# The third map set of a gateless tick moves behind the rounds

## The chip, the cores and the metric

The kernel runs on one core of one Trainium2 chip. The metric is the device time of one execution in microseconds (us); the figure given is the median of several runs. Engines are named as the profile names them: PE (matmul), PEld (weight load), DVE, ACT, POOL and SP, which here only starts transfers.

## What is computed

The input `x` is 8 images of 8 channels and 512 x 512 points in float32. Two layers follow each other, each of the form x + f(group_norm(x)). Layer 0 is a spectral convolution on a grid of half the resolution that keeps 4 x 4 modes. Layer 1 has three branches and a blend of them:

```python
grid = drive                                  # 1: "map", 15 steps, each channel by itself
for _ in range(15):
    mapped = R * grid * (1.0 - grid)
    local = conv3x3_per_channel(mapped, K_local)
    grid = (1 - BETA) * ((1 - EPS) * mapped + EPS * local) + BETA * drive
cml = clip(grid, 1e-4, 1 - 1e-4)
h = relu(conv3x3(x, Wp) + bp)                 # 2: "nca", 8 -> 128 channels
nca = sigmoid(conv1x1(h, Wu) + bu)            #    128 -> 8 channels
gin = concat(x, cml, nca)                     # 3: "gate", 24 -> 8 -> 8 channels
g = sigmoid(conv1x1(relu(conv3x3(gin, Wg1) + bg1), Wg2) + bg2)
out = x + g * cml + (1 - g) * nca
```

## The kernel before, in words

An image is an *element*. Its work is cut into small pieces, and the source issues the pieces in an order written out by hand; the last call of the kernel (`keep_order`) makes every engine follow the order of the source. The unit of that order is the *tick*, one call of `turn` (L1145), which calls `work` (L1084).

**Map sets.** The rows of an image are cut into overlapping slabs of 32 rows, so that 15 steps can run in on-chip memory. A set (`Slabs`, L493) holds 16 slabs of one channel or pairs of four channels: the state `m`, and two layouts of the drive, `dE` for even and `dO` for odd steps. Nine sets make an element: four sets of channels 0 to 3 (first phase), then four of channels 4 to 7 and a `Tail` set (second phase). The list `slots` orders them: step 1 of every set of the phase, step 2 of every set, and so on. A tick takes `TICK` = 3 slots. One slot is

- `convolve` (L541): 48 matmuls in the source, 96 in the trace, into one *half* of the accumulators. There are two halves of two tiles `pair` each, and `half()` (L1088) takes them in turn.
- `settle` (L554): DVE adds the drive to one tile of the half (L560), ACT squares the result (L566), then both again for the other tile. It is a generator that stops before the second square. The square, and what follows it, run when it is next called: the drive's own preparation on POOL after step 1 (`drive(0)`, L539), the release of a drive tile at steps 14 and 15 (`sets.drop(d)`), the clip at step 15 (L619), and `renew` (L578), which exchanges edge rows between neighbouring sets by four transfers that POOL starts (L593, L594).

**Rounds.** `Hidden.round` (L738) makes four rows of `h`: 24 matmuls in the trace (L746) into a half, then ACT evicts one tile of it (L752) and DVE the other (L754). A tick has one to three rounds. The second call of the last set's `settle` lies in the first round.

**Channel sums.** `Hidden.point` (L769) multiplies the new rows of `h` by `Wu`, 8 matmuls a round in the trace (L773), and collects four rounds in a tile `y`: the first group of them is copied by ACT (L780), later ones are added by DVE (L782), and the fourth is followed by a sigmoid (L785) and a store (L788). When a tick's rounds fall into two groups of four, there are two calls, into the two sides of the same tile `pair`.

**Gates and spectral pieces.** A gate (`Gate`, L795) does 12 rows of the blend of the element before, and a *piece* is a step of layer 0 for the element after. A tick takes them up where they are due, around the sums.

**A tick before the change**, in the order of every engine: three map sets; then `transfers` (L1105); then the rounds; `squares` (L1114); then sums, gate and pieces; then `tick()`, which issues stores put off (the map's result, `cml`, L623), and `squares` again.

**Transfers and slots.** `transfers` (L1149) issues on SP, in this order, the store of `y`, up to two loads of 1 MB of the next image (`x`, L184), and the loads of the drives of the next phase (`Phase.fetch`, L710; four loads of 256 KB a tile, L518). A drive tile is loaded only if

```python
if not h and sets.room() <= begun - self.squared or len(s.e.closed) < C:
    break
```

lets it pass: `room()` is the number of free slots, `begun` counts the sets of the phase that have begun, and `squared` those whose state exists. The slots are 19 in all, of which 16 are for sets in the last four ticks of a phase. `square` (L520) makes the state from `dE` on ACT (L525) and takes a slot. `prepare` (L698) calls `drive(1)` at the start of a tick, four instructions on POOL (L539) that scale `dO` in place; it takes a tile that was loaded in an earlier tick. Step 1 of a set reads `dO`.

Of the kernel before, what the change touches and what calls it, by code (L numbers as in the profile page):

```python
# [54 lines left out]
TICK = 3  # L55
WIDE, EARLY, FILL, LATE, LAST = "wide", "early", "fill", "late", "last"
# [63 lines left out]
def conv_layers(ctx: ExitStack, tc: tile.TileContext, a, out):  # L120
# [45 lines left out]
    def later(ticks, work):  # L166
        put_off.append((now[0] + ticks, work))

    def tick(end=False):
        now[0] += 1  # L170
        due = [w for at, w in put_off if end or at <= now[0]]
        put_off[:] = [] if end else [(at, w) for at, w in put_off if at > now[0]]
        for work in due:
            work()
# [504 lines left out]
    class Phase:  # L679
# [23 lines left out]
        def squares(self, n):  # L703
            while self.squared < len(self.sets) and sets.room():
                if not self.ready(self.squared, 0, n + TICK):
                    break
                self.sets[self.squared].square()
                self.squared += 1
# [86 lines left out]
    class Gate:  # L795
# [59 lines left out]
        def finish(self):  # L855

            x1, o = (self.mix[: GR * C, q] for q in range(2))
            nc.vector.scalar_tensor_tensor(  # L858
                o, o, self.e.back[: GR * C, 0:1], x1, ALU.add, ALU.add
            )  # L860
            self.store()
# [71 lines left out]
    class Others:  # L933
# [52 lines left out]
        def busy(self):  # L986
            ahead = self.loaded or self.begun
            return self.before.gates or ahead or self.convolved or self.pointed

        def finish(self):  # L990
            while self.pointed:
                self.pointed.popleft().finish()
# [64 lines left out]
    others = Others()  # L1057
    for n in count():
# [6 lines left out]
        ps = next(turns)  # L1065
# [18 lines left out]
    def work(steps, rounds, e, after, gates, transfers, squares=lambda: None):  # L1084

        double = gates == 2 and not others.lag

        def half():  # L1088
            used[0] += 1
            return halves[used[0] % 2]  # L1090

        settled = iter(())
        for n, (s, step) in enumerate(steps):
            ps = half()
            s.convolve(step, ps)
            next(settled, None)
            settled = s.settle(step, ps)
            next(settled)
            others.finish()
            if gates == 2 and shared.most < 6:  # L1100
                others.load(1)
                gates = 1
        if steps:
            others.finish()
        transfers()  # L1105
        if steps:
            had = len(others.loaded) + len(others.begun)
            others.load(gates, early=True)
            gates -= len(others.loaded) + len(others.begun) - had
        for _ in range(rounds):  # L1110
            e.hidden.round(half(), after, settled)
        next(settled, None)
        others.finish()
        squares()  # L1114


        first, second = halves[used[0] % 2], halves[(used[0] + 1) % 2]
        if not others.spectral(WIDE, second):
            used[0] += 1
            first, second = second, first  # L1120
        groups = e.hidden.sums()
        gate = others.ready()
        if not gate:
            others.spectral(EARLY, [first[0][:, 0]])
        if len(groups) == 2:
            e.hidden.point(groups.pop(0), first[1][:, 0])
        two = False
        if gate:
            others.conv(first[0][:, 0])
            others.spectral(EARLY, [second[0][:, 0]])  # L1130
            two = others.ready(double)
            if two:
                others.conv(second[0][:, 0])
        if groups:
            e.hidden.point(groups[0], first[1][:, 1])
        others.spectral(FILL, [None])
        others.spectral(LATE, [second[1][:, 0]])
        others.point()
        others.spectral(LAST, [first[1][:, 0]])
        used[0] += two  # L1140
        others.load(gates)
        tick()
        squares()
# [26 lines left out]
    for b in range(B):  # L1170
# [3 lines left out]
        done, rounds = e.hidden.n, ROUNDS if after else ROUNDS_LAST  # L1174
        first, second = phases[2 * b : 2 * b + 2]
# [98 lines left out]
```

## Time and profile before

| what | value |
|---|---|
| median of 3 runs | 9159.09 us (9153.91 to 9171.87) |
| the profiled execution's own time | 9170.25 us |
| its span, first to last instruction | 9168.5 us |
| mean granted TensorE clock | 0.991 |
| PE busy | 8748.3 us (95%) |
| DVE busy | 5628.9 us (61%) |
| ACT busy | 4099.4 us (45%) |
| POOL busy | 3383.3 us (37%) |
| map matmuls, L547 | x103680, 3681.8 us |
| round matmuls, L746 | x24576, 2779.2 us |
| sum matmuls, L773 | x8192, 996.2 us |

Busy times are unions of the instructions' spans. In the views of groups, a row has the line, the engine, the operation, what it writes and reads, its shape and count, then the busy time and the mean duration of one, then the idle time of that engine just before, with what ended most of it. In a timeline a row is the start (us from the first instruction), the length, engine, line, operation, operands and count of instructions merged into it, and in brackets the idle time before it and what ended it. "issue" means that nothing in the profile explains the idle time.

### The profile page before, as it was taken

The numbers are of one execution on the slowest core, as the hardware profiler recorded it, in microseconds if no ns is written. First come the engines' busy times: TensorE is split into PE (matmuls) and PEld (weight loads), VectorE is DVE, ScalarE is ACT, GpSimd is POOL, SyncE is SP. The second block draws the span as 40 slices with busy tenths as digits, with TensorE's granted clock in tenths as the row PEclk, the third lists the DMA queues.
The fourth block names the chain that finished last, engine by engine and source line by source line (L and its number), as shares of the span: only waits on it lengthen the run. The fifth ranks groups of instructions, "written<-read, shape, count | busy, mean of one in ns | idle before, by whom it ended". The sixth has DMA issues, their size and how long they took to land. (4 is left out here: it accounts for less than half of the span.)

```text
span 9168.5 us, 334776 instructions
## 1 busy us (share of the span) xinstructions
PE 8748.3 (95%) x150992; PEld 4141.6 (45%) x150992; DVE 5628.9 (61%) x5844; ACT 4099.4 (45%) x4285; POOL 3383.3 (37%) x4470
## 2 busy tenths in 40 slices
PE   5999999999999999999999999999999999999999
PEld 2445544444444444444444444444444444444433
DVE  6665567555675567655676556765567655565654
ACT  2455544444444444444444444444444444444432
POOL 3242434324343243433434334343333434454423
PEclk9999999999999999999999999999999999999999
DMA  5241356745566455754557545565465754755587
GB/s 161 81 133 39 108 138 176 171 110 140 145 179 162 112 157 140 186 143 113 155 150 180 140 113 155 155 174 140 113 164 150 180 135 106 177 138 140 118 209 204
DMA packets 695939, 1327.27 MB, mean 145 GB/s; under 512 B 147648, under 2 KB 153152, under 8 KB 667024
## 3 DMA queue, kind: packets, MB, share of 16 engines
q1 hardware_dynamic: 587376, 1235.73, 52.5%
q0 software_dynamic: 104992, 69.33, 3.5%
q8 instruction: 1187, 19.45, 0.9%
q14 instruction: 240, 1.97, 0.1%
q10 hardware_dynamic: 2144, 0.80, 0.0%
HBM read 977.48 MB, written 270.61 MB: 136 GB/s over the span
## 5 line engine op out<-in xcount | busy, mean ns | idle before, releaser
L547 PE MATMUL pair<-m,band 32*32 32x512 f32 x103680 | 3681.8, 604 | 178.4 <-issue 113.3
L566 ACT ACTIVATE m<-m 128x1024 f32<-128x1024 f32 x2016 | 2128.7, 1056 | 2038.6 <-DVE m L560 1963.9
L547 PEld LDWEIGHTS pair<-m,band 32*32 32x32 f32 x103680 | 2141.5, 103 | 1650.2 <-issue 785.9
L746 PE MATMUL pair<-cols,w_p 32*128 32x511 f32 (+1 forms) x24576 | 2779.2, 597 | 22.9 <-DMA cols<-xn 15.1
L754 DVE TENSOR_SCALAR h<-pair,b_p 128x1024 f32<-128x1024 f32 x1024 | 1313.6, 1283 | 1135.9 <-PE pair L746 1125.8
L593 POOL DMA_DIRECT2D m<-m x1568 | 851.0, 543 | 3087.7 <-ACT m L566 3012.8
L746 PEld LDWEIGHTS pair<-cols,w_p 32*128 32x128 f32 x24576 | 1308.8, 185 | 1501.8 <-issue 1157.3
L560 DVE SCALAR_TENSOR_TENSOR m<-pair,dO 128x1024 f32<-128x1024 f32 x1152 | 1356.2, 1219 | 982.0 <-PE pair L547 791.1
L560 DVE SCALAR_TENSOR_TENSOR m<-pair,dE 128x1024 f32<-128x1024 f32 x1008 | 1186.8, 1219 | 862.3 <-PE pair L547 671.3
L752 ACT ACTIVATE h<-pair,b_p 128x1024 f32<-128x1024 f32 x1024 | 1141.1, 1114 | 1184.9 <-PE pair L746 1174.2
L853 POOL TENSOR_TENSOR mix<-mix 96x512 f32<-96x512 f32 x344 | 437.3, 1277 | 1853.1 <-ACT mix L851 1806.1
L773 PE MATMUL pair<-h,w_u 128*32 128x512 f32 x8192 | 996.2, 596 | 72.3 <-DVE y L782 45.7
L830 PE MATMUL pair<-gin,w_g 128*32 128x511 f32 (+1 forms) x8256 | 951.6, 597 | 21.4 <-DMA gin<-nca 11.7
L594 POOL DMA_DIRECT2D m<-m x1568 | 838.0, 534 | 55.1 <-issue 31.7
L773 PEld LDWEIGHTS pair<-h,w_u 128*32 128x32 f32 x8192 | 246.0, 109 | 684.7 <-issue 523.7
L830 PEld LDWEIGHTS pair<-gin,w_g 128*32 128x32 f32 x8256 | 252.5, 110 | 669.5 <-issue 599.0
L785 ACT ACTIVATE y<-y,b_u 128x512 f32<-128x512 f32 x256 | 184.8, 722 | 727.4 <-DVE y L782 727.4
L835 POOL TENSOR_TENSOR mix<-mix 96x512 f32<-96x512 f32 x344 | 443.7, 1292 | 139.6 <-DMA mix<-nca 86.7
L780 ACT COPY y<-pair 128x512 f32<-128x512 f32 x256 | 149.9, 586 | 641.3 <-PE pair L773 622.7
L570 POOL TENSOR_SCALAR dO<-dO 128x2048 f32<-128x2048 f32 x72 | 398.0, 5527 | 95.3 <-DVE m L560 94.4
L847 PE MATMUL pair<-mix,w_g 128*32 128x512 f32 x2064 | 354.4, 601 | 44.1 <-DVE mix L840 40.6
L840 DVE TENSOR_SCALAR mix<-pair,b_g 128x512 f32<-128x512 f32 x344 | 257.1, 747 | 222.6 <-PE pair L830 213.4
(96 smaller groups left out, 3038.9 us busy)
## 6 DMA issues: line engine op xcount, KB each, us to landing
gin<-xn SPq DMA_DIRECT2D x344, 384.0 KB
x<-in_x SPq DMA_DIRECT2D x120, 1024.0 KB
cols<-xn SPq DMA_DIRECT2D x240, 512.0 KB
gin<-cml SPq DMA_DIRECT2D x344, 320.0 KB
gin<-nca SPq DMA_DIRECT2D x344, 320.0 KB
dE<-xn SPq DMA_DIRECT2D x288, 256.0 KB
dO<-xn SPq DMA_DIRECT2D x288, 256.0 KB
mix<-xn SPq DMA_DIRECT2D x344, 192.0 KB
```

Source lines behind the costliest of these rows:

```text
L547: nc.tensor.matmul(ps[h // 2][32 * t : 32 * t + 32, h % 2], band[at, self.channel(step - 1, h, t), dx], m[at, t, dx : dx + N], start=(n == ...
L560: nc.vector.scalar_tensor_tensor(u[:, at], ps[q], FLOOR, d[:, at], ALU.max, ALU.add)
L566: nc.scalar.square(u[:, at], u[:, at])
L593: nc.gpsimd.dma_start(out=view(tb, rb, dims), in_=view(ta, ra, dims))
L594: nc.gpsimd.dma_start(out=view(ta, ra + s, dims), in_=view(tb, rb + s, dims))
L746: nc.tensor.matmul(ps[g // 2][:, g % 2, lo:hi], w_p[p, dx, i % 2], self.cols[p, i // 2, at : at + hi - lo], start=(n == 0), stop=(n == 2), ...
L752: nc.scalar.activation(h[:, :2], ps[0], AF.Relu, bias=b_p)
L754: nc.vector.tensor_scalar(h[:, 2:], ps[1], b_p, 0.0, ALU.add, ALU.max)
L773: nc.tensor.matmul(ps[32 * g : 32 * g + 32], w_u[:, r % 4], h[:, g], start=(r == hs[0][0]), stop=(r == hs[-1][0]), tile_position=(0, 32 * g),)
L830: nc.tensor.matmul(ps[32 * j : 32 * j + 32, lo:hi], gband[:, dx], gin[:, j, at : at + hi - lo], start=(n == 0), stop=(n == 2), tile_positi ...
L835: nc.gpsimd.tensor_tensor(d, d, ng, ALU.subtract)
L853: nc.gpsimd.tensor_tensor(d, d, mix[: GR * C, 2], ALU.mult)
```

## The change

A tick is *idle* for the other elements when no spectral piece of the element after is left and no gate is loaded and due. In an idle tick of three map sets and at least one round, the third set is taken out of the list and run, with both calls of its `settle` at once, after the rounds and before the second `squares`, the sums and the end of the tick. The sums then always take the half that the last round used, and not the half of the late set.

```diff
@@ class Others
+        def idle(self):
+            return not (self.after and self.after.pieces) and not self.ready()
+
@@ def work
+        late = []
+        if len(steps) == TICK and rounds and not double and others.idle():
+            steps, late = steps[:-1], steps[-1:]
         settled = iter(())
         for n, (s, step) in enumerate(steps):
             ps = half()
...
             e.hidden.round(half(), after, settled)
         next(settled, None)
         others.finish()
+        for s, step in late:
+            ps = half()
+            s.convolve(step, ps)
+            for _ in s.settle(step, ps):
+                pass
         squares()
 
 
         first, second = halves[used[0] % 2], halves[(used[0] + 1) % 2]
-        if not others.spectral(WIDE, second):
+        if late or not others.spectral(WIDE, second):
             used[0] += 1
             first, second = second, first
```

## Prediction, made before the run

> **What bounds the kernel now.** I read first the page's table of busy time:
>
> ```profile
> span 9168.5 us, 334776 instructions
> ...
> PE 8748.3 (95%) x150992; PEld 4141.6 (45%) x150992; DVE 5628.9 (61%) x5844; ACT 4099.4 (45%) x4285; POOL 3383.3 (37%) x4470
> ```
>
> PE is the bound; whatever lengthens its order, or lets it stand, is paid. Then I stepped the source's rules tick by tick. Of 360 ticks with three sets, 60 meet the new condition: 28 in element 0 (the last 28, since no element before it has gates), 4 in each of elements 1 to 6 (one late in the first phase, the last three of the second), 8 in element 7. By rounds and groups of sums: 22 have three rounds in one group, 15 have groups of two and one, 6 of one and two; 14 have two rounds, 3 have one. The timeline of PE shows three of these shapes in a row:
>
> ```profile
> 794.42 9.75 PE L547 MATMUL pair<-m,band 32*32 32x512 f32 x288
> 804.11 8.00 PE L746 MATMUL pair<-cols,w_p 32*128 32x512 f32 x72
> 812.03 2.78 PE L773 MATMUL pair<-h,w_u 128*32 128x512 f32 x24
> 814.75 9.75 PE L547 MATMUL pair<-m,band 32*32 32x512 f32 x288
> 824.43 5.43 PE L746 MATMUL pair<-cols,w_p 32*128 32x512 f32 x48
> 829.78 1.07 PE L773 MATMUL pair<-h,w_u 128*32 128x512 f32 x8
> 831.40 1.06 PE L773 MATMUL pair<-h,w_u 128*32 128x512 f32 x8 [0.56 <-ACT h L752]
> 832.40 9.75 PE L547 MATMUL pair<-m,band 32*32 32x512 f32 x288
> 842.08 8.00 PE L746 MATMUL pair<-cols,w_p 32*128 32x512 f32 x72
> 850.01 1.92 PE L773 MATMUL pair<-h,w_u 128*32 128x512 f32 x16
> 852.83 1.06 PE L773 MATMUL pair<-h,w_u 128*32 128x512 f32 x8 [0.90 <-DVE y L782]
> ```
>
> Three rounds in one group: no wait, 20.33 us a tick. Two rounds: the sums wait 0.56 us for the last eviction, 17.65. Two groups: the second waits 0.90 us for DVE to read the first out of the same tile, 21.43. So all there is to win in clean ticks is 0.56 us in 14 of them and 1.2 in 3. What the late set adds on DVE:
>
> ```profile
> 804.21 2.35 DVE L560 SCALAR_TENSOR_TENSOR m<-pair,dE 128x1024 f32<-128x1024 f32 x2 [0.84 <-PE pair L547]
> ```
>
> The two reads start 0.04 us after the set's last matmul (804.17) and end at 806.56: 2.4 us in which its half isn't free. Last, the transfers before an element's end (SP, POOL, SP):
>
> ```profile
> 2217.13 2.01 SPq L518 DMA_DIRECT2D dE<-xn  x4
> 2220.05 3.50 SPq L518 DMA_DIRECT2D dO<-xn  x4
> ```
> ```profile
> 2232.60 2.72 POOL L539 TENSOR_SCALAR dO<-dO,base 128x512 f32<-128x512 f32 x4 [6.38 <-DMA dO<-xn]
> ```
> ```profile
> 2251.69 4.58 SPq L184 DMA_DIRECT2D x<-in_x  x2
> ```
>
> The last drive tile of the next phase (set 3's dO) is issued until 2223.55; POOL has it at 2232.60, 9.1 us later. SP starts the next image's first two loads at 2251.69, as the element's second tick (2251.83) begins.
>
> [...] The page's queue q8 moved 19.45 MB in 1187 packets, 16.4 KB each[...]. [...] after 2.46 us of waiting (and 0.73 shortly before) three rounds took 10.27 us, not 8.00:
>
> ```profile
> 5595.65 3.09 PE L547 MATMUL pair<-m,band 32*32 32x512 f32 x37 [2.46 <-issue]
> 5598.67 10.27 PE L746 MATMUL pair<-cols,w_p 32*128 32x512 f32 x72
> ```
>
> **The change, part by part.**
>
> *A. The split run of sets.* In single instructions a first set takes 2.82 us to the next, a second 3.12, a third 3.75 to the rounds: 9.69. Split, two take 2.82 + 3.12 + 0.5 (the drain into rounds) = 6.44, and a set alone 2.80 + 0.51 = 3.31: 9.75. The added switch costs 0.07 us a tick.
>
> *B. The new waits.* The next tick's first set takes the late set's half, so it starts no sooner than 2.5 us after the late set ends; and DVE, in order, adds y only after those two reads. Per shape, before to after:
> - three rounds, one group: sums of 2.72 us cover 2.5. +0.07 (the switch) x 22 = 1.5.
> - two rounds: the 0.56 us goes, but sums of 1.8 us leave 0.8 to the half. 17.52 to 17.67 in the commonest tick: +0.15 x 14 = 2.1. One round: the same, +0.05 x 3 = 0.2.
> - groups of two and one: DVE's y (0.69 us) ends 3.1 us after the late set, then 1.14 us to the next set as now: the sums' stretch grows from 3.82 to 4.30. +0.55 x 15 = 8.3.
> - one and two: the y add now comes right after 8 matmuls and 16 follow it: 4.04 to 5.16. +1.19 x 6 = 7.1.
>
> A and B together: **+19 us**. Weight loads and rounds wait for nothing new: each round's half was read out a matmul block earlier, as before. [...]
>
> *C. Transfers move.* The second set's release of its drive tile, in the second call of `settle`, used to run before `transfers`; now it runs in the first round, after it. One slot fewer is seen. I stepped the slots through the last three ticks of a second phase. First: room 2, loads set 0's dO and set 1's dE; now room 1, only dO. Second: room 2, set 1's dO and set 2's dE; now room 3, set 1's dE and dO, then room 1 isn't above begun 2 - squared 1. Third: room 4, squared 3, set 2's dO, set 3's dE and dO; now room 5 but squared 2: set 2's dE, dO, set 3's dE, and then 2 isn't above 4 - 2. So set 3's dO is issued one tick later, in the next element's first tick, behind two image loads, and `drive(1)` for it goes to the start of the second tick. That tick's first set is set 3's step 1, which needs it. By the lines above: SP ends the images at 2256.27, four issues 2.3, then 6.5 to 9.1 us to POOL: 2265 to 2268. Four drives 2.72, DVE 2.4: 2270.2 to 2272.8. The tick's third map set needs that half and would start at 2251.83 + 5.97 = 2257.80. It stands 12.4 to 15 us, say 13.7, and then runs cold for about 2.3 (10.27 - 8.00). **+16 us** at each of the six element boundaries that load an image; at the seventh (7858.6) no image is ahead, I take 13. Sum +109. Unknown is the landing: 10 us a boundary if it lands early, 20[...].
> At the half phases of elements 0 and 7, the same load slips by one tick, ahead of the Tail's two: POOL's drive starts behind the late set's exchange. +3 each, 0 to 6: **+6**.
>
> *D. Gaps that move.* In the 60 ticks PE also stands for instructions and others at the third set (the rows of 5595.65; 6.3 us at 7829, 5 at 8691, 2.7 at 8243, six of 0.5 to 2). [...] Single ticks give 34 us with the cold rounds, of which 17 lie just before a boundary, where C's load fixes the end anyway. I count 0.7 of the other 17: **-12**.
>
> Sum: 19 + 109 + 6 - 12 = +122 on the profiled execution's 9170.25 (span 9168.5 and 1.75 around it): 9292. The runs' median is 11 lower: **9280** after rounding, +1.3%. What is late next at a boundary: the late map set's own release sets the rounds, which follow without a further stop.
>
> **The rivals.** 0.2% is about what a measurement here can tell from no change (18 us).
> 1. *Only the local order counts.* The loads arrive in time, since the DMA share is 0.56 in the first tick of an element (table of stretches, 2234.1 to 2251.8); D gives nothing. 9159 + 19 = 9178. Against it: SP itself stands 6.38 us on a store before the images, so it can't be early.
> 2. *Not slower: the gaps are filled.* [...] all 34 us return, 19 are paid, 9144. It decides only if set 3's dO is driven before about 2257 at each boundary; it needs C to be nil.
> 3. *The condition hardly holds*, say in element 0 alone: 28 ticks of +0.3, about 9168.
> 4. *Worse:* the standing tick pushes gates and later loads, or SP is held a second time: 20 us or more a boundary, 9360.
>
> **Chances.** Forecast 0.78, rivals 0.08, 0.06, 0.02, 0.06. The forecast's own range: 7 x 10 + 10 + 0 - 34 = +46 to 7 x 20 + 28 + 12 = +180, 9205 to 9339; ends that need everything at once are rare, and the local cases lie below, so 9190 to 9335. Faster by over 0.2%: 0.04; within: 0.08; slower: 0.88.
>
> **What would show it.** A: two L547 runs a tick, 192 and 96. B: the bracket before the second L773 group at 1.4 instead of 0.90 (2.2 instead of 1.12 in groups of one and two), and before L547 0.8 after two rounds. C: SP's L518 four times after L184 in the first tick of elements 1 to 6; POOL's L539 dO in the second tick ended by that DMA; PE's L547 idle 12 to 15 us there. If those gaps are under 5 us the prediction is wrong. D: no gap at 7829 and 5584.

## The result and the profile after

| version | median, us | lowest to highest, runs | profiled execution (span) | ratio to before, 95% interval |
|---|---|---|---|---|
| before | 9159.55 | 9153.91 to 9171.87, 4 | 9170.25 (9168.5) | |
| after | 9282.74 | 9275.36 to 9285.35, 4 | 9285.35 (9283.1) | 1.0129, 1.0116 to 1.0141 |

The change makes the kernel 1.3% slower; 9280 had been forecast. The mean granted TensorE clock went from 0.991 to 0.986.

The page of the changed kernel, from the table of busy time:

```profile
PE 8789.2 (95%) x150992; PEld 4093.4 (44%) x150992; DVE 5640.9 (61%) x5844; ACT 4093.4 (44%) x4285; POOL 3375.5 (36%) x4470
```

PE has the same 150992 matmuls and 40.9 us more of busy time, so part of the loss is in matmuls that take longer and the rest in waits. The view of PE's waits names them (what waits for whom: sum in us, times, longest):

```profile
PE pair L547 <- issue: 111.5, 73, 4.7
PE pair L773 <- DVE y L782: 68.2, 35, 2.9
PE pair L547 <- DVE m L560: 66.1, 9, 11.8
```

Before, these three were 113.3, 45.7 and 13.6 (65, 35 and 7 times). Sets that wait for DVE's drive add (L560) are the large new item: 65.4 of the 66.1 us lie in seven waits, one in the second tick of each element but the first. The sums' wait for `y` grew by 22.5 us over the same 35 waits.

**A clean tick.** The timeline of PE, a tick of two rounds and, from 774.79, the start and the second group of sums of a tick of groups of two and one:

```profile
757.73 6.58 PE L547 MATMUL pair<-m,band 32*32 32x512 f32 x192
764.24 5.43 PE L746 MATMUL pair<-cols,w_p 32*128 32x512 f32 x48
769.60 3.41 PE L547 MATMUL pair<-m,band 32*32 32x512 f32 x96
772.93 1.92 PE L773 MATMUL pair<-h,w_u 128*32 128x512 f32 x16
774.79 7.24 PE L547 MATMUL pair<-m,band 32*32 32x512 f32 x192
...
796.45 1.06 PE L773 MATMUL pair<-h,w_u 128*32 128x512 f32 x8 [1.30 <-DVE y L782]
```

The sets stand as 192 and 96. After two rounds the sums run 16 matmuls without a stop (the 0.56 us is gone), but the next run of sets takes 7.24 us, not 6.58. Inside that run its first set waits 0.66 us for the late set's half, which DVE reads until 775.43. The second group of sums waits 1.30 us instead of 0.90.

**An element boundary.** The timelines of SP, POOL and PE around the second tick of the next element, which starts at 2277.87 here and started at 2251.83 before:

```profile
2273.14 1.58 SPq L184 DMA_DIRECT2D x<-in_x  x2
2274.77 3.58 SPq L518 DMA_DIRECT2D dO<-xn  x4
```
```profile
2292.22 2.70 POOL L539 TENSOR_SCALAR dO<-dO,base 128x512 f32<-128x512 f32 x4 [14.92 <-DMA dO<-xn]
```
```profile
2277.87 6.48 PE L547 MATMUL pair<-m,band 32*32 32x512 f32 x180
2287.97 1.08 PE L547 MATMUL pair<-m,band 32*32 32x512 f32 x12 [3.62 <-issue]
2294.90 6.35 PE L547 MATMUL pair<-m,band 32*32 32x512 f32 x96 [5.85 <-DVE m L560]
```

Read from the bottom: the third set starts 17.03 us into the tick (5.97 before) because DVE had no drive to add; POOL had none to scale until 2292.22; and SP issued that load, the four L518, only in the element's first tick, behind two image loads of 1 MB each. The 3.62 us put down to "issue" is a wait for instructions inside the same standing time (the last section has the reason to read it so); without it the wait for DVE is one piece, 10.1 to 11.8 us long at five other boundaries. The set then takes 6.28 us to the rounds (L746 starts at 2301.18), 3.75 before. The tick is 38.09 us long, before 23.77.

**Where the time went.** I cut both traces into ticks and subtracted:

| part of the 114.6 us between the spans | us |
|---|---|
| seven second ticks of elements (12.7 to 14.7 each) | +97.4 |
| 15 idle ticks, groups of two and one | +24.8 |
| 6 idle ticks, groups of one and two | +9.7 |
| 22 idle ticks of three rounds | -11.1 |
| 14 of two rounds | -6.7 |
| 3 of one round | -7.2 |
| all other ticks | +7.8 |

### The profile page after: what moved, and what is told of

The parts are those of the page before. It is cut to its first block, busy times and chain, and to the rows that moved or that the text cites. A ratio compares the mean times of both kernels' runs of the same rounds, so it can differ in the third digit from the quotient of the medians.

```text
span 9283.1 us, 334727 instructions
## 1 busy us (share of the span) xinstructions
PE 8789.2 (95%) x150992; PEld 4093.4 (44%) x150992; DVE 5640.9 (61%) x5844; ACT 4093.4 (44%) x4285; POOL 3375.5 (36%) x4470
## 5 line engine op out<-in xcount | busy, mean ns | idle before, releaser
L547 PE MATMUL pair<-m,band 32*32 32x512 f32 x103680 | 3723.9, 606 | 221.8 <-issue 111.5
L547 PEld LDWEIGHTS pair<-m,band 32*32 32x32 f32 x103680 | 2101.7, 103 | 1769.7 <-issue 837.9
L746 PE MATMUL pair<-cols,w_p 32*128 32x511 f32 (+1 forms) x24576 | 2778.9, 596 | 36.7 <-DMA cols<-xn 14.8
L560 DVE SCALAR_TENSOR_TENSOR m<-pair,dO 128x1024 f32<-128x1024 f32 x1152 | 1356.7, 1219 | 1104.7 <-PE pair L547 775.6
L746 PEld LDWEIGHTS pair<-cols,w_p 32*128 32x128 f32 x24576 | 1303.5, 185 | 1523.6 <-issue 1156.2
L560 DVE SCALAR_TENSOR_TENSOR m<-pair,dE 128x1024 f32<-128x1024 f32 x1008 | 1186.5, 1218 | 886.6 <-PE pair L547 726.8
L773 PE MATMUL pair<-h,w_u 128*32 128x512 f32 x8192 | 998.0, 599 | 87.5 <-DVE y L782 68.2
L830 PE MATMUL pair<-gin,w_g 128*32 128x511 f32 (+1 forms) x8256 | 952.1, 598 | 24.3 <-DMA gin<-nca 14.4
L773 PEld LDWEIGHTS pair<-h,w_u 128*32 128x32 f32 x8192 | 243.0, 110 | 703.9 <-issue 558.6
```

Source lines behind the costliest of these rows:

```text
L547: nc.tensor.matmul(ps[h // 2][32 * t : 32 * t + 32, h % 2], band[at, self.channel(step - 1, h, t), dx], m[at, t, dx : dx + N], start=(n == ...
L560: nc.vector.scalar_tensor_tensor(u[:, at], ps[q], FLOOR, d[:, at], ALU.max, ALU.add)
L746: nc.tensor.matmul(ps[g // 2][:, g % 2, lo:hi], w_p[p, dx, i % 2], self.cols[p, i // 2, at : at + hi - lo], start=(n == 0), stop=(n == 2), ...
L773: nc.tensor.matmul(ps[32 * g : 32 * g + 32], w_u[:, r % 4], h[:, g], start=(r == hs[0][0]), stop=(r == hs[-1][0]), tile_position=(0, 32 * g),)
L830: nc.tensor.matmul(ps[32 * j : 32 * j + 32, lo:hi], gband[:, dx], gin[:, j, at : at + hi - lo], start=(n == 0), stop=(n == 2), tile_positi ...
```

## The experiments

Theory: nearly all of the loss comes from the release of a drive tile that slips past `transfers`, and so from one load a boundary. Rivals: the loss comes from the new order on PE itself; or from the queue order on SP, images ahead of the load. The first four share one chip, on which before took 9165.02 us; the last two share another, with 9168.25.

| kernel | median, us (runs) | ratio to before, 95% interval | PE's L547 waits for DVE's m | PE's L773 waits for DVE's y |
|---|---|---|---|---|
| release first | 9187.61 (17) | 1.0028, 1.0021 to 1.0035 | 0.6 us | 67.9 us |
| one slot fewer | 9311.20 (4) | 1.0161, 1.0148 to 1.0175 | 124.8 | 45.8 |
| drive before images | 9259.23 (4) | 1.0105, 1.0091 to 1.0118 | 41.4 | 68.2 |
| release first, two tiles | 9158.18 (13) | 0.9990, 0.9981 to 0.9998 | 0.6 | 25.5 |
| two tiles only | 9150.23 (13) | 0.9983, 0.9974 to 0.9991 | 10.5 | 25.5 |
| late at the end, two tiles | 9142.67 (13) | 0.9976, 0.9968 to 0.9984 | 10.9 | 25.5 |

**1. The release first.** The changed kernel, with the second set's second `settle` call put back ahead of `transfers`. The late set stays behind the rounds. The call brings the set's second square and its edge exchange forward too, and not the release alone; the second experiment changes the slots alone.

```diff
         if steps:
             others.finish()
+        if late:
+            next(settled, None)
         transfers()
```

> The changed order of the sets, but the second set's settle is finished before the transfers, so that they see the slots that they saw before. If the late load is the cause of the loss (theory): the seven stalls of 12 to 15 us in an element's second tick are gone, set 3's dO is issued in the last tick of the element before, and the time is 9160 to 9185 us, some 100 us under the changed kernel. If the order of the sets itself, or the wait for its half, costs the time (rival): 9250 us or more.

Measured: 1.0028; the median of 9187.61 us is 3 us above the range that was given. The profiled execution took 9179.38 us. Of the seven boundary stalls nothing is left (the seven ticks differ from before by 7.2 us in all, not 97.4). The same boundary, SP's last drive loads and then PE:

```profile
2239.39 4.65 SPq L518 DMA_DIRECT2D dO<-xn  x4
...
2266.20 4.60 SPq L184 DMA_DIRECT2D x<-in_x  x2
```
```profile
2272.60 10.49 PE L547 MATMUL pair<-m,band 32*32 32x512 f32 x288
```

The drive is issued 22 us ahead of the images again, and the three sets of the second tick run as one. Two lines of source take the ratio from 1.0129 to 1.0028. What stays, 23 us by the medians, comes with the rest of the new order. Its profiled execution is only 9 us over that of before: its idle ticks have +21.1 in groups of two and one, +8.8 in one and two, and -21.3 in the others. The profiled execution is 8 us under this version's median and that of before 5 us over its own on this chip, which makes up the difference. Which ticks vary from run to run is open, for there is one profile of each.

**2. One slot fewer, old order.** The kernel before, with nothing moved, but `transfers` sees one free slot fewer in those idle ticks in which the second set is at step 14 or later.

```diff
+        fewer = 0
+        if len(steps) == TICK and rounds and not double and others.idle():
+            fewer = int(steps[1][1] >= STEPS - 1)
...
+        sets.most -= fewer
         transfers()
+        sets.most += fewer
```

> The order of before, unchanged; only the transfers of the idle ticks whose second set is at step 14 or 15 see one slot fewer, as in the changed kernel. Theory: the load slips as in the changed kernel, seven stalls of 12 to 15 us, 9250 to 9275 us. Rival (the order costs the time): within 10 us of before.

Measured: 1.0161, more than the change itself. The direction is as expected; the size is not (9250 to 9275 us had been given). SP and PE at the boundary, whose second tick starts at 2273.85:

```profile
2276.42 1.91 SPq L184 DMA_DIRECT2D x<-in_x  x2
2278.39 3.63 SPq L518 DMA_DIRECT2D dO<-xn  x4
```
```profile
2297.53 6.87 PE L547 MATMUL pair<-m,band 32*32 32x512 f32 x96 [17.10 <-DVE m L560]
```

The images are issued 2.57 us into the tick, where the changed kernel has them 4.73 us ahead of it, and the third set starts at +23.68 instead of +17.03. The seven ticks lose 132.8 us. So the slot alone makes the stall, without any late set. The late set even shortens it: SP's load of `cols` (L729) starts within 0.1 us of the end of a tick's rounds at this boundary in all three versions, and the stores ahead of the images follow it. In the changed kernel the late set and the sums come after that point, so it lies 25.3 us ahead of the second tick; 20.6 us here, 20.2 us before.

**3. The drive before the images.** The changed kernel; a drive load that slipped into the next element is issued ahead of that tick's images.

```diff
+            for p in now_phases:
+                if at >= p.at:
+                    p.fetch(at)
             if others.after:
                 others.after.fetch()
             for p in now_phases:
-                p.fetch(at)
+                if at < p.at:
+                    p.fetch(at)
```

> The changed kernel, but a drive load that is still due when its phase has begun is issued on SP ahead of the two image loads. Theory: at six boundaries 2 MB less lie ahead of set 3's dO[...]; POOL's drive starts 6 to 7 us after the last issue instead of 14, the stall falls from about 12 to 5 us, and the cold stretch shrinks: 9225 to 9250 us. Rival (the load is late because of the stores ahead of it, or POOL is late for another reason): within 10 us of the changed kernel.

Measured: 1.0105, 23 us under the changed kernel by the medians and above the range of 9225 to 9250 us that was given; the seven boundary ticks give back 28 us. SP and POOL, where the second tick starts at 2274.07:

```profile
2271.24 3.09 SPq L518 DMA_DIRECT2D dO<-xn  x4
2274.50 1.12 SPq L184 DMA_DIRECT2D x<-in_x  x2
```
```profile
2284.68 2.70 POOL L539 TENSOR_SCALAR dO<-dO,base 128x512 f32<-128x512 f32 x4 [11.17 <-DMA dO<-xn]
```

The last of the four loads is issued at +0.26 us (+0.48 in the changed kernel): SP gained almost nothing, since the store of `nca` holds it for 8.53 us here too. What shrank is the way from that issue to POOL, 10.35 us instead of 13.87. It had been expected to shrink to 6 or 7 us. So the images ahead in the queue cost 3.5 us at this boundary (over the six boundaries that load an image the third set starts 4.8 us sooner in the mean); the rest of the stall comes with the slipped tick itself.

**4. Two tiles for the two groups.** The kernel of experiment 1, and the second group of sums goes to the half's other tile, so that it need not wait until DVE has read the first.

```diff
-            e.hidden.point(groups[0], first[1][:, 1])
+            e.hidden.point(groups[0], first[0][:, 1] if late else first[1][:, 1])
```

> e1_release_first, and in ticks with a late set the second group of sums goes to the other tile of the half, so that it doesn't wait for DVE to read the first. Theory (the added wait in ticks of two groups is DVE's y behind the late set's two reads): 21 ticks lose 1.3 to 2.4 us each, 25 to 40 us under e1_release_first, 9125 to 9150 us. Rival (the next set's wait for its half takes the place of that wait at once): within 10 us of e1_release_first.

Measured: 0.9990, 29 us under the kernel of experiment 1. The absolute time lies above the range that was given, the step is as expected. A tick of groups of two and one, PE:

```profile
788.48 2.78 PE L773 MATMUL pair<-h,w_u 128*32 128x512 f32 x24
791.19 6.58 PE L547 MATMUL pair<-m,band 32*32 32x512 f32 x192
```

All 24 matmuls of the sums run without a stop. PE's wait for `y` falls from 67.9 to 25.5 us, 42 us; in its one profile 20 us of that come back as waits for instructions (93.3 to 113.8 us).

**5. Two tiles only.** The same edit in the kernel before, without a late set.

```diff
+        alone = len(steps) == TICK and not double and others.idle()
...
-            e.hidden.point(groups[0], first[1][:, 1])
+            e.hidden.point(groups[0], first[0 if alone else 1][:, 1])
```

> The kernel before with no late set; only in ticks without gate and pieces the second group of sums goes to the other tile. Theory (PE waits 0.9 to 1.1 us there for DVE to read a tile of which the other side is free): 21 ticks lose 1.1 to 1.4 us, 20 to 27 us in all, 9130 to 9142 us, ratio about 0.997. Rival (the next map sets wait for the second tile instead): within 5 us of before.

Measured: 0.9983, 18 us under before, less than expected. The wait for `y` goes from 45.7 to 25.5 us, so that 20 us was to be had. With the late set (0.9990, experiment 4) the kernel is not seen to be faster than without it; the two intervals overlap, so no gain of the late set beyond the second tile is shown.

**6. The late set where gaps are.** The kernel of experiment 5; the late set runs behind the rounds only in the last tick of each second phase (`Tail` at step 15), with the release first as in experiment 1. The diff shows the new condition, against the kernel before; the late loop is that of the change. The trace of before has long waits for instructions in several of these ticks (2.46 us at 5595.65 among them).

```diff
+        late = []
+        alone = len(steps) == TICK and rounds and not double and others.idle()
+        if alone and isinstance(steps[-1][0], Tail) and steps[-1][1] == STEPS:
+            steps, late = steps[:-1], steps[-1:]
```

> e5_two_tiles_only, and the late set only in the last tick of each element's second phase (8 ticks), its releases as before. Theory (there PE stands for instructions during the third set, up to 6 us with a cold clock behind it, and the rounds give them time): 10 to 20 us under e5_two_tiles_only, 9112 to 9130 us. Rival (the instructions or transfers that are late there are late in the next tick instead): within 5 us of e5_two_tiles_only, or above it.

Measured: 0.9976, the lowest ratio of all, 7.6 us under the kernel of experiment 5, where 10 to 20 had been expected; the intervals of the two overlap, so the size of that step is unsure. The last tick of element 1, first in the kernel of experiment 5 and then here, PE:

```profile
2208.80 1.75 PE L547 MATMUL pair<-m,band 32*32 32x512 f32 x7 [4.91 <-issue]
```
```profile
2206.71 2.13 PE L547 MATMUL pair<-m,band 32*32 32x512 f32 x39 [0.46 <-issue]
2208.78 8.00 PE L746 MATMUL pair<-cols,w_p 32*128 32x512 f32 x72
```

With the third set behind the rounds the 4.91 us is not there. The seven such ticks that another element follows take 20.8 to 22.3 us; in experiment 5 they took 21.0 to 28.7 and before 21.0 to 29.2. But the rival is in part in the same traces: against experiment 5 these seven ticks are 13.3 us shorter together, and the seven that follow them 8.6 us longer.

## Why the prediction was right

The sum foretold +122 us on the profiled execution; it was +115. By its own steps:

- **A, the split, +0.07 us a tick:** +0.17 in the commonest tick of three rounds (20.49 us, before 20.33). Shown, and of no weight.
- **B, the new waits.** The bracket ahead of the second group is 1.30 (foretold 1.4) in six ticks of two and one, 1.40 in a seventh, and 2.07 (foretold 2.2) in those of one and two. Three clean ticks in a row lose 0.93 us, 0.77 by the sum. Two things are missing from the step. In eight of the 15 ticks of two and one, those near a phase's end, the late set is at step 15, and its clip (L619) also stands ahead of `y` on DVE, as in this one:

```profile
7944.65 1.23 DVE L619 TENSOR_SCALAR m<-m 128x2048 f32<-128x2048 f32 x1
7945.80 0.68 DVE L782 TENSOR_TENSOR y<-y,pair 128x512 f32<-128x512 f32 x1
```

  The bracket in the eight is 2.56 to 2.92 us. At 1.3 us each that is 10 us that the step did not count. The second is the clock. Of the 14 brackets that are now over 2 us (these eight and the six of 2.07), nine have a stretch of 3.41 us at half the granted clock right behind them; before, at 0.90 and 1.12 us, none was. This is the row of the stretches for one of them, behind the bracket of 2.56 us that ends at 2235.44 (the third number from the end is the granted clock):

```profile
2234.90:2238.30 3.40, 2.86 (x40) 0.65 (x41) 0.39 (x1) 1.52 (x4) 2.69 (x4) 0.50 0.98 367
```

  By an estimate from these figures (9 times half of 3.41) it costs up to 15 us in this profile. Another of the nine is seen under D, where the first run of sets takes 8.13 us instead of 6.58.
  The late set's exchange of edge rows adds no wait that is seen: PE's waits at L547 for `m` from a DMA come to 6.3 us, 8.3 before. Such transfers took 4.9 and 5.4 us from issue to landing (medians of the two sizes).
- **C, one slot fewer.** The slipped load, its place behind two image loads, POOL's late drive and the standing third set are all in the trace. The first experiment shows that this cause is needed, the second that it suffices. 109 us were foretold for the seven boundaries, 15.6 each; 97.4 were measured, 13.9 each. Three terms inside it were wrong, and the first two cancel. SP was to end the images 4.4 us into the tick, as before (the first rival was held unlikely because SP could not be early), and ended them 3.2 us ahead of it, 7.6 us earlier. The landing was to take 6.5 to 9.1 us after the last issue (POOL in the trace of before: 2217.03 to 2223.50, and 2223.55 to 2232.60) and took 13.87. The early start also held the four issues up: 3.58 us, not 2.3. POOL so began at +14.35 us, inside the window of 13.2 to 15.8 that the sum had given: that is luck, since neither error was foreseen. The third term was too large. From POOL's start to the third set the sum had 5.1 us (2.72 for four drives, then 2.4 for DVE), and it took 2.68. DVE starts 1.40 us after POOL, with two of the four drives done, and PE starts with the first of DVE's two instructions done:

```profile
2293.62 2.57 DVE L560 SCALAR_TENSOR_TENSOR m<-pair,dO 128x1024 f32<-128x1024 f32 x2 [16.79 <-POOL dO L539]
```

  So the third set stands 11.06 us here, and 10.9 to 12.9 us at the six boundaries with an image, where 12.4 to 15 had been foretold. The seventh boundary, which has no image, took 14.4 us (13 foretold); there POOL began 9.3 us after the last issue.
- **The cold set, 2.3 us:** 6.28 against 3.75 us, 2.5. The granted clock was 0.50 from 2289.52 to 2299.76, over most of that set. Half clock followed shorter waits too. The prediction's own example, a wait of 2.46 us, has 6.83 us at a granted clock of 0.50 behind it, from 5596.47 on. In the trace of before, 25 of the 43 waits of PE of 2 to 3 us between 160 and 8650 us were followed within 7 us by a stretch at half clock, and 6 of the 46 of 1 to 2 us.
- **The half phases of elements 0 and 7, +6:** about nothing. This term was too large.
- **D, gaps filled, -12.** That a set behind the rounds finds its instructions there was the author's estimate. The idle ticks together lost 9.4 us, where A, B and D together foretold 7. By the clean values A and B are 35, without the clock's share (22 x 0.17; 14 x 0.20 after two rounds, -0.46 in the tick and +0.66 in the next; 15 x 0.56, 1.22 less that 0.66; the clip's 10; 9.7 in the six of one and two), so about 25 us of gaps or more were filled, of the 34 that were there. Both terms were too small, and nearly cancel. The step put the 17 us just ahead of a boundary at nothing, because C's load was to fix the end there. That reason failed: the images are issued some 20 us behind the rounds of that last tick, before the change and after, so they moved with it. The seven last ticks became 15.1 us shorter; but the seven first ticks behind them became 8.9 us longer, and these are in the last row of the table. One of the last ticks, which had 2.46 us of waiting and cold rounds, PE in the changed kernel:

```profile
5665.37 8.13 PE L547 MATMUL pair<-m,band 32*32 32x512 f32 x192
5673.43 8.24 PE L746 MATMUL pair<-cols,w_p 32*128 32x512 f32 x72
5681.60 3.41 PE L547 MATMUL pair<-m,band 32*32 32x512 f32 x96
```

It went from 28.0 to 23.25 us, the one at 7829 from 29.25 to 20.74. But PE's waits for instructions at L547 are 111.5 us as a whole, 113.3 before: others appeared elsewhere, so a filled gap is not simply a gain. That they move with every version is seen; why is not settled.

Of the rivals, the one of the local order alone is what the first experiment built: 19 us over before foretold, 22.6 measured by the medians. The one that needed C to be nil is refuted by the same kernel: even without C the gaps don't pay for the waits. The third was off from the start: the condition holds in 60 ticks, in every element. The fourth didn't come: no boundary lost more than 14.7 us. That the images' place in the queue is the main cause is refuted by the third. What makes up the 10.35 us from the last issue to POOL when nothing but stores is ahead was not tried.

## What to carry to other kernels

When a step moves in an order written by hand, list everything that it releases, not only what it computes: here a counter read a moment too early cost ten times what the new order on the bounding engine cost in the same profile. Look first for such a release, for putting it back takes two lines. A wait that a new order makes longer (PE for `y`) may be better taken away at its root: here a second tile in the old order brought 18 us. What the new order adds to that is not clear of the noise, even where it fills a gap that the trace shows (experiments 4 to 6); look at the next tick too before you count such a gap as won.

## What was not expected of the hardware

- The way from the last of four 256 KB issues to POOL's first use: 13.87 us with 2 MB of image loads just ahead in the same queue, 10.35 us with the image loads behind, 9.3 us with none. So the loads ahead cost time, 3.5 us between the first two; in what order the queue carries out what SP has issued, no run shows.
- SP stands on the single store of `nca` for 6.38 us (before), 8.07 (after) and 9.43 (one slot fewer), for the same 256 KB. SP's next issue starts 0.3 us after its end in all three; what sets its length was not tried.
- PE's waits at L547 that the views call "issue" come to 93 to 131 us in every version, but at different ticks in each; a change of order that removes one can bring another. This alone makes steps of 10 us hard to tell apart from one profile. That they are waits for instructions is how I read the traces: before and after, every such wait longer than 0.5 us (57 and 59) ended 1.2 to 1.8 us after a packet of 16.4 KB on the instruction queue q8 had ended; of moments taken at random, 8% lie so.
- In the changed kernel PE's granted clock fell to half after waits far shorter than the stalls at the boundaries, nine times behind brackets of 2.07 to 2.67 us ahead of the second group of sums. Experiment 1 has the same 14 brackets over 2 us, and five such stretches behind them (1.5 to 1.7 us more in the matmuls there); so how often it happens differs from one profile to another.
